# A transformer block in fp32 on one Trainium2 core: GpSimd in program order through the first attention, its factor work in pieces, and sums kept in order

## The chip, the core and the metric

The kernel runs on one core of a Trainium2 chip. A core has a matrix engine (TensorE, PE in the profile, with its weight loads as PEld), a vector engine (VectorE, DVE), an activation engine (ScalarE, ACT), a general engine (GpSimd, POOL), and a queue engine that issues the DMAs here (SyncE, SP). Each engine takes its own instructions one after the other; semaphores make one wait for another. The metric is the device time of one execution in microseconds (us). The kernel before took 2533.49 us (median of three runs, 2530.73 to 2535.2). About 0.2% of it, 5 us, is what such a measurement can tell from no change.

## The reference

The input x is 2 x 1024 x 1024 in fp32. Four parts follow one another, each on the layernorm of x and added to x:

```python
x = x + attn_a(layernorm(x))   # 32 heads of 32, causal, rotary, a prefix of 10 adapter rows
x = x + ffn(layernorm(x))      # x @ W_base.T + b, plus 8 experts of rank 16 mixed by sparsemax
x = x + attn_b(layernorm(x))   # 8 heads of 16, not causal
x = x + ffn(layernorm(x))
```

The change touches the first, whose core is

```python
q, k, v = split(einsum('btc,oc->bto', x, w_attn), 3)      # 1024 -> 3 * 1024
rotary(t) = t * cos + concat([-t[16:], t[:16]]) * sin     # q and k, per head
y = softmax(where(causal, q k^T / sqrt(32), -inf)) v
y = y + gating * softmax(q ak^T / sqrt(1024)) av          # ak, av: adapter rows through w_attn
return y @ w_proj.T
```

## The kernel before

**Stages.** `stage_a` is the first attention for both batches (about the first 1250 us). Then come its output projection, the first feed-forward part, the second attention and the last feed-forward part, one laid into the other. Only `stage_a` and the helper `Filler` are touched.

**Units and half-steps.** `attend` works off 32 units of `stage_a`: batch b (2), group g of four heads (8), half n of the 1024 queries (2). A unit needs scores twice. First `sc` = q k^T (L297), of which DVE takes the row minimum of the negated scores (L310, `nmax` and `part`), and ACT the sum of exponentials (L318); at the unit's end ACT takes a logarithm (L325) and six small DVE operations (L335 to L340, `shift`) split the shift of each row into three bf16 parts. Then, two steps later, `st` = k q^T transposed with the shift added as a bf16 matmul (L365, L367), ACT's exponential into `pt` (L478), GpSimd's causal mask on the diagonal blocks of `pt` (L374), and `y_A` += v pt (L389). `attend` runs through this in half-steps, some 290 in all, each with the `sc` of one unit and the `st` of an earlier one; both use the same two PSUM buffers in turn, so a late minimum holds up the scores behind it. The adapter scores (L708 to L726) and their small softmax are done per unit on DVE, ACT and GpSimd (`aw`, L726).

**Fill.** Between half-steps TensorE does dense work: the projections of the units to come. `Filler` holds them as generators; each `yield` says how many nanoseconds a matmul is worth (HF * COL = 870 for 128 x 512), and after each half-step `fill.run` steps the generator until `FILL_A` is paid. What is not done by the end of stage A is done behind it.

**Projections in seven products.** From group 1 on a projection of a 2 x 2 block matrix is made with seven products in place of eight (`seven`, L618), in the order 1, 6, 2, 7, 5, 4, 3, each of four matmuls (L198 or L196 in the profile, outputs `x`, `y` and `z`; `x_v`, `y_v`, `z_v` for values). Weight combinations are made by GpSimd: `factors` (s1, s2 and one in place, L608 to L610, six operations of 128 x 256) and `last_factor` (L616, two operations), which product 3 needs. Input combinations are made once for each batch: `combine` writes twelve tiles, t3 and t2 by DVE (L581, L582), t4 by GpSimd (L586), to DRAM `td`, from which a `Stream` reads them back through five buffers; `combine_first` (L600) makes another in place on GpSimd. Sums of products are taken by DVE (L636 to L654). Finished parts of q and k go to `rotate` (L770): DVE shuffle (L775), DVE times cos (L776), GpSimd times sin (L777), GpSimd add (L778), all 128 x 512.

**Order.** TensorE runs in the order in which the program is written; the others are ordered by the scheduler, where `keep_in_program_order` ties an instruction behind the one of its engine that was written before it.

Of the kernel before, what the change touches and what calls it, by code (L numbers as in the profile page):

```python
# [20 lines left out]
P = 128  # L21
# [3 lines left out]
HF = 512  # L25
# [10 lines left out]
COL = 1.7  # L36
FILL_A = 2080.0
FILL_B = 2650.0, 2200.0
# [10 lines left out]
class Filler:  # L49
# [4 lines left out]
    def __init__(self):  # L54
        self.gens = deque()
        self.done = set()
        self.debt = 0.0
        self.spent = 0.0
        self.at = {}
        self.ahead = 0  # L60

    def add(self, gen, gate=None):
        self.gens.append((gen, gate))

    def step(self, cold=True):
        while self.gens:
# [19 lines left out]
            if isinstance(r, tuple):  # L86
                self.done.add(r)
                self.at[r] = self.spent
                continue
            self.spent += r  # L90
            return r
        return None
# [44 lines left out]
def tile_model(ctx: ExitStack, tc: tile.TileContext, d, out: bass.AP):  # L137
# [379 lines left out]
    def stage_a(wk, big):  # L517
# [31 lines left out]
        def block(b, i):  # L549

            k, n = divmod(i, 10)
            return xnT[b, n - 1][:, 4 * (k - 1) : 4 * k, :]
# [21 lines left out]
        streams = {}  # L574

        def combine(b):

            for c in range(4):
                b11, b12, b21, b22 = (block(b, i)[:, c, :] for i in (11, 12, 21, 22))
                t3, t2, t4 = (big.tile([P, HF], F32, tag="tt", name=f"tn{b}_{i}_{c}") for i in (3, 2, 4))  # L580
                dve.tensor_sub(t3, b22, b12)  # L581
                dve.tensor_add(t2, t3, b11)  # L582
                sp.dma_start(td[b, 3, c], t3)
                sp.dma_start(td[b, 2, c], t2)
                for h in range(0, HF, 2 * P):
                    pool.tensor_sub(t4[:, h : h + 2 * P], t2[:, h : h + 2 * P], b21[:, h : h + 2 * P])  # L586
                sp.dma_start(td[b, 4, c], t4)

            order = []
            for g in range(NG):  # L590
                order += [2, 3, 4] if g else []
                if g > 1 or b:
                    order += [4] if g % 2 else [2, 3]
            streams[b] = Stream(b, order)

        def combine_first(b):
            for c in range(4):
                t1, b11 = block(b, 12)[:, c, :], block(b, 11)[:, c, :]
                for h in range(0, HF, 2 * P):
                    pool.tensor_sub(t1[:, h : h + 2 * P], t1[:, h : h + 2 * P], b11[:, h : h + 2 * P])  # L600

        def factors(w, tag, nm):


            s1, s2 = (wk.tile([P, 4, P], F32, tag=tag, name=f"s{i}_{nm}", bufs=2) for i in (1, 2))
            for c in range(0, 4, 2):
                cs = slice(c, c + 2)
                pool.tensor_add(s1[:, cs], w[21][:, cs], w[22][:, cs])  # L608
                pool.tensor_sub(s2[:, cs], s1[:, cs], w[11][:, cs])
                pool.tensor_sub(w[21][:, cs], w[11][:, cs], w[21][:, cs])  # L610
            return {1: w[11], 2: w[12], 3: w[12], 4: w[22], 5: s1, 6: s2, 7: w[21]}

        def last_factor(f):
            for c in range(0, 4, 2):
                cs = slice(c, c + 2)
                pool.tensor_sub(f[3][:, cs], f[3][:, cs], f[6][:, cs])  # L616

        def seven(b, nm, f, mul, shape, c, first, settled):  # L618

            stream = streams[b]
            right = {1: lambda k: block(b, 11)[:, k, :], 2: lambda k: block(b, 21)[:, k, :], 3: lambda k: block(b, 22)[:, k, :],
                     4: lambda k: stream.get(4, k), 5: lambda k: block(b, 12)[:, k, :],
                     6: lambda k: stream.get(2, k), 7: lambda k: stream.get(3, k)}

# [5 lines left out]
            yield from product(1, x, stop=False)  # L632
            act.copy(c[22], x)
            y = block_bank(shape, f"y6_{nm}", 1)
            yield from product(6, y)
            dve.tensor_add(c[12], c[22], y)  # L636
            yield from product(2, x, start=False)
            first(x)
            y = block_bank(shape, f"y7_{nm}", 1)
            yield from product(7, y)  # L640
            last_factor(f)
            dve.tensor_add(c[21], c[12], y)
            yield None
            z = block_bank(shape, f"z_{nm}")
            yield from product(5, z, stop=False)
            dve.tensor_add(c[22], c[21], z)
            settled(22)
            y = block_bank(shape, f"y4_{nm}", 1)
            yield from product(4, y)
            dve.tensor_sub(c[21], c[21], y)  # L650
            settled(21)
            yield True
            yield from product(3, z, start=False)
            dve.tensor_add(c[12], c[12], z)  # L654
            settled(12)
# [91 lines left out]
        def adapter_parts(nm, weights, n):  # L747

            ap = bank([P, n], f"ap_{nm}")
            for c in range(NC):  # L750
                i = 32 * (c % 4)
                pe.matmul(ap[i : i + 32], lhsT=adT[:, c, :], rhs=weights(c), start=(c < 4), stop=(c >= 4), skip_group_check=True)
            parts_at[nm] = wk.tile([P, n], F32, tag="qr", name=f"parts_{nm}", bufs=2)
            evac(parts_at[nm], ap)
# [15 lines left out]
        def rotate(b, g, key, n, src):  # L770
# [5 lines left out]
            dve.tensor_mul(qT, src, cos[:, cols])  # L776
            pool.tensor_mul(qr, qr, sin[:, cols])  # L777
            pool.tensor_add(qT, qT, qr)  # L778

# [480 lines left out]
    with tc.manual_schedule(engines={mybir.EngineType.PE}):  # L1260
        with tc.tile_pool(name="big", bufs=2, side="left", reuse_waits="tile") as bigp:
# [3 lines left out]
            with tc.tile_pool(name="wkA", bufs=5, side="right", reuse_waits="tile") as wk:  # L1265
                wp = stage_a(PoolOf(wk, {"pr": 6, "qk": 6, "pt": 4}), big)
            fill.drain()
# [143 lines left out]
```

## Time and profile before

| | us |
|---|---|
| three runs | 2530.73, 2533.49, 2535.2 |
| the profiled execution | 2534.4 |
| its span in the trace | 2532.7 |
| mean granted TensorE clock | 0.992 |
| stage A, 20 to 1250: TensorE busy | 1175.57 of 1230 |
| first product L777 and add L778 of q, 128 x 512 on GpSimd | 1.78 and 1.28 |
| a factor or combination, 128 x 256 on GpSimd | 0.73 to 0.89 |
| a row minimum over 512, DVE | 0.69 to 0.75 |

How to read the lines shown below. A window has its bounds, its length, then busy time and instruction count for TensorE, weight loads, DVE, ACT and GpSimd, the granted TensorE clock (1 is full speed), the DMA share and GB/s. A wait names the engine that waited, its tile and line, the engine, tile and line that it waited for, the time in all, how often, and the longest. A timeline line has its start, its duration, engine, line, operation, output <- inputs, shapes and count, and in brackets the idle time before it and what ended it.

### The profile page before, as it was taken

The page shows a single profiled execution, that of the slowest core. Times are in us where ns is not written, and L with a number is a line of the kernel's source. Part 1 is how long each engine was busy: PE and PEld are TensorE (multiplying, and loading weights), DVE is VectorE, ACT ScalarE, POOL GpSimd, SP SyncE. Part 2 cuts the span into 40 slices and gives each one's busy share as a digit, 9 for nine tenths or more (in the row PEclk, how much of TensorE's full clock was granted, in tenths as well). Part 3 has the DMA queues.
Part 4 walks back from the last instruction along what each step waited for, and adds up shares of the span by engine and source line. Part 5 has one row for each costly group of instructions (what it writes and reads, how often), then busy time and mean ns, then how long its engine had stood idle before and what let it go on. Part 6 is the DMA issues. An engine that isn't in the chain of part 4 may idle for free.

```text
span 2532.7 us, 60644 instructions
## 1 busy us (share of the span) xinstructions
PE 2448.0 (97%) x25597; PEld 1102.8 (44%) x25597; DVE 1282.1 (51%) x4036; ACT 1093.9 (43%) x2085; POOL 586.4 (23%) x840
## 2 busy tenths in 40 slices
PE   7999999999899999999999999999999999999999
PEld 4434434444354444445433445566333563333344
DVE  7665555556555555555530113357555765654243
ACT  2336656565465665556642000011354525555200
POOL 2342343333324334333200001100100101111120
PEclk9999999999999999999999999999999999999999
DMA  6532322323323333223312461121001311212121
GB/s 210 204 88 77 102 76 89 98 81 93 126 81 107 92 105 93 86 85 84 120 63 70 154 217 54 50 90 45 34 34 35 126 35 34 93 43 83 44 100 42
DMA packets 142513, 224.36 MB, mean 89 GB/s; under 512 B 12832, under 2 KB 73376, under 8 KB 142240
## 3 DMA queue, kind: packets, MB, share of 16 engines
q1 hardware_dynamic: 142240, 220.48, 27.0%
q8 instruction: 200, 3.28, 0.5%
q14 instruction: 73, 0.60, 0.1%
HBM read 168.01 MB, written 52.43 MB: 87 GB/s over the span
## 4 chain that ended last, share of the span: by engine, by line
PE 82%; DVE 6%; ACT 5%; POOL 3%; DMA 3%; issue 1%; SPq 0%; ACTq 0%; POOLq 0%; DVEq 0%
PE fo_f L196 11%; PE st L367 9%; PE fo_f L198 8%; PE sc L297 6%; PE op L196 6%; PE y_A L389 5%; PE y L198 4%; PE z L198 4%; PE op L198 3%; PE st L365 3%; PE x L198 3%; PE y_B L389 2%; PE y_v L198 2%; ACT pr_A L318 2%; PE bq L196 2%; PE z_v L198 2%
## 5 line engine op out<-in xcount | busy, mean ns | idle before, releaser
L478 ACT ACTIVATE pt<-st 128x1024 f32<-128x1024 f32 (+1 forms) x418 | 426.3, 1020 | 650.9 <-PE st L367 481.2
L318 ACT ACTIVATE pr_A<-pr_A,nmax_A 128x896 f32<-128x896 f32 (+7 forms) x512 | 390.0, 765 | 71.9 <-DVE nmax_A L310 71.5
L310 DVE CUSTOM_DVE_ANT_0 pr_A<-sc,mask 128x512 f32<-128x512 f32 (+3 forms) x512 | 250.9, 536 | 198.1 <-PE sc L297 103.4
L297 PE MATMUL sc<-kT,qT 32*128 32x512 f32 (+3 forms) x1536 | 329.4, 526 | 13.8 <-DVE nmax_A L310 8.1
L367 PE MATMUL st<-qT,kT 32*128 32x512 f32 (+3 forms) x1536 | 309.2, 489 | 0.0
L214 POOL TENSOR_TENSOR xf<-xf,b_base 128x256 f32<-128x256 f32 x128 | 89.3, 730 | 759.4 <-DVE xn_f L236 456.2
L196 PE MATMUL fo_f<-wb,xt_f 128*128 128x512 f32 x548 | 248.1, 596 | 0.4 <-ACT hwT_f L1117 0.4
L310 DVE CUSTOM_DVE_ANT_0 pr_A<-sc,mask,part_A 128x512 f32<-128x512 f32 (+1 forms) x256 | 156.1, 647 | 158.2 <-PE sc L297 100.9
L198 PE MATMUL fo_f<-wb,xt_f 128*32 128x512 f32 x1904 | 226.9, 595 | 0.1
L374 POOL TENSOR_SCALAR_AFFINE_SELECT pt<-pt 128x256 f32<-128x256 f32 x256 | 100.0, 409 | 460.3 <-ACT pt L478 460.3
L389 PE MATMUL y_A<-pt,v 128*32 128x512 f32 (+3 forms) x1536 | 166.7, 502 | 13.6 <-POOL pt L374 13.6
L318 ACT ACTIVATE pr_B<-pr_B,nmax_B 128x1024 f32<-128x1024 f32 x128 | 145.6, 1140 | 30.9 <-DVE nmax_B L310 30.8
L196 PEld LDWEIGHTS fo_f<-wb,xt_f 128*128 128x128 f32 x548 | 101.6, 193 | 111.2 <-issue 110.6
L297 PE MATMUL sc<-kq,qk 32*128 32x512 f32 x512 | 144.3, 640 | 2.7 <-DVE nmax_B L310 2.3
L367 PE MATMUL st<-rows_B,kq 32*128 32x512 f32 x512 | 144.3, 640 | 0.2 <-ACT pt L478 0.2
L196 PE MATMUL op<-wp,yt 128*128 128x512 f32 x334 | 143.9, 592 | 0.0
L228 ACT ACTIVATE lv_f<-ve_f 128x1 f32<-128x1 f32 x32 | 6.5, 203 | 315.7 <-DVE ve_f L226 315.7
L365 PE MATMUL st<-rows_A,ones 3*128 3x512 bf16 (+3 forms) x768 | 128.0, 330 | 13.5 <-DVE nmax_A L310 13.5
L367 PEld LDWEIGHTS st<-qT,kT 32*128 32x128 f32 x1536 | 133.7, 186 | 16.3 <-issue 11.3
L310 DVE CUSTOM_DVE_ANT_0 pr_B<-sc,mask,part_B 128x512 f32<-128x512 f32 x128 | 91.1, 746 | 78.8 <-PE sc L297 78.7
L297 PEld LDWEIGHTS sc<-kT,qT 32*128 32x128 f32 x1536 | 113.8, 185 | 30.9 <-DVE nmax_A L310 12.3
L365 PEld LDWEIGHTS <-ones 3*128 3x128 bf16 x768 | 36.9, 91 | 199.3 <-issue 191.9
(272 smaller groups left out, 3741.6 us busy)
## 6 DMA issues: line engine op xcount, KB each, us to landing
tt<-td SPq DMA_DIRECT2D x252, 256.0 KB, 2.8
wqk<-in_w_attnT SPq DMA_DIRECT2D x32, 512.0 KB, 5.2
xf<-x SPq DMA_DIRECT2D x32, 512.0 KB, 3.3
xa<-in_x SPq DMA_DIRECT2D x16, 512.0 KB, 6.4
wv<-in_w_attnT SPq DMA_DIRECT2D x8, 1024.0 KB, 5.4
yd<-ys SPq DMA_DIRECT2D x32, 256.0 KB, 2.5
yt<-yd SPq DMA_DIRECT2D x128, 64.0 KB, 2.0
xp<-in_x SPq DMA_DIRECT2D x32, 256.0 KB, 2.9
```

The source lines that it names most:

```text
L196: return pe.matmul(out, lhsT=lhsT, rhs=rhs, start=start, stop=stop, skip_group_check=True)
L198: pe.matmul(out[i : i + 32], lhsT=lhsT[:, i : i + 32], rhs=rhs, start=start, stop=stop, skip_group_check=True)
L214: pool.tensor_add(dst[:, i : i + 2 * P], a[:, i : i + 2 * P], b[:, i : i + 2 * P])
L228: act.activation(lv, ve, AF.Ln)
L297: yield w * COL, lambda: pe.matmul(dst[:, o : o + w], lhsT=self.qt[rows, qc : qc + P], rhs=self.kt[rows, c0 : c0 + w], start=True, stop=True)
L310: dve.tensor_tensor_reduce(pr[:, c0 : c0 + w], sc[:, i, o : o + w], m, -self.scale, BIG if c0 == 0 else self.part[:, col], ALU.add, ALU.mi ...
L318: tc.keep_in_program_order(act.activation(pr[:, :nk], pr[:, :nk], AF.Exp, bias=self.nmax[:, col], scale=-1.0, accum_out=self.sums[:, col]))
L365: yield w * COL / 4, lambda: pe.matmul(dst[:, o : o + w], lhsT=ones[three, :], rhs=self.rows[three, off : off + w], start=True, stop=False)
L367: yield w * COL, lambda: pe.matmul(dst[:, o : o + w], lhsT=self.kt[rows, kb * P : (kb + 1) * P], rhs=rhs, start=self.extra, stop=True)
L374: pool.affine_select(out=dg, in_=dg, compare_op=ALU.is_ge, fill=0.0, base=0, pattern=[[0, 2], [1, P]], channel_multiplier=-1)
L389: pe.matmul(self.y[32 * h : 32 * h + 32, off : off + w], lhsT=self.value(h, kb), rhs=pt[h // 2][:, h % 2, o : o + w], start=self.opens, st ...
L478: act.activation(pt[:, :, low_:wide_], st[:, :, low_:wide_], AF.Exp, scale=ts[0][0].scale)
```

## The change

- `Filler` gets a queue of small pieces (`chores`); after each step of dense work one of them is written out, and `flush` writes out all that are left.
- `combine`, `combine_first`, `factors` and `last_factor` put their operations into that queue. Each combined tile is made and stored as a piece of its own, and the stream is opened by the last piece. The factors come in the order s1, s1, s2, s2, and the one in place.
- In `seven` the queue is flushed before product 6 and before product 3; `last_factor` is called behind product 5, no longer behind product 7; the five sums, and DVE's t3 and t2, are kept in program order.
- `rotate` takes the two GpSimd operations in halves of 128 x 256, as four.
- `parts` gets a buffer of its own in place of one of the `qr` buffers.
- `stage_a` is built with GpSimd in program order.
- `FILL_A` goes from 2080 to 2040.

```diff
@@ -34,7 +34,7 @@
 NEG = -1e30
 BIG = 3e38
 COL = 1.7
-FILL_A = 2080.0
+FILL_A = 2040.0
 FILL_B = 2650.0, 2200.0
 SETTLE = 4500.0
 RING = 5
@@ -58,6 +58,11 @@
         self.spent = 0.0
         self.at = {}
         self.ahead = 0
+        self.chores = deque()
+
+    def flush(self):
+        while self.chores:
+            self.chores.popleft()()
 
     def add(self, gen, gate=None):
         self.gens.append((gen, gate))
@@ -88,6 +93,8 @@
                 self.at[r] = self.spent
                 continue
             self.spent += r
+            if self.chores:
+                self.chores.popleft()()
             return r
         return None
 
@@ -573,56 +580,67 @@
 
         streams = {}
 
+        def in_pieces(op):
+            def both(dst, x, y):
+                for h in range(0, HF, 2 * P):
+                    op(dst[:, h : h + 2 * P], x[:, h : h + 2 * P], y[:, h : h + 2 * P])
+            return both
+
+        def pin_sub(*a):
+            tc.keep_in_program_order(dve.tensor_sub(*a))
+
+        def pin_add(*a):
+            tc.keep_in_program_order(dve.tensor_add(*a))
+
+        def made(ts, b, i, c, op, x, y):
+            t = ts[i, c] = big.tile([P, HF], F32, tag="tt", name=f"tn{b}_{i}_{c}")
+            op(t, x, y)
+            sp.dma_start(td[b, i, c], t)
+
         def combine(b):
 
+            ts = {}
             for c in range(4):
                 b11, b12, b21, b22 = (block(b, i)[:, c, :] for i in (11, 12, 21, 22))
-                t3, t2, t4 = (big.tile([P, HF], F32, tag="tt", name=f"tn{b}_{i}_{c}") for i in (3, 2, 4))
-                dve.tensor_sub(t3, b22, b12)
-                dve.tensor_add(t2, t3, b11)
-                sp.dma_start(td[b, 3, c], t3)
-                sp.dma_start(td[b, 2, c], t2)
-                for h in range(0, HF, 2 * P):
-                    pool.tensor_sub(t4[:, h : h + 2 * P], t2[:, h : h + 2 * P], b21[:, h : h + 2 * P])
-                sp.dma_start(td[b, 4, c], t4)
+                fill.chores.append(lambda c=c, x=b22, y=b12: made(ts, b, 3, c, pin_sub, x, y))
+                fill.chores.append(lambda c=c, y=b11: made(ts, b, 2, c, pin_add, ts[3, c], y))
+                fill.chores.append(lambda c=c, y=b21: made(ts, b, 4, c, in_pieces(pool.tensor_sub), ts[2, c], y))
 
             order = []
             for g in range(NG):
                 order += [2, 3, 4] if g else []
                 if g > 1 or b:
                     order += [4] if g % 2 else [2, 3]
-            streams[b] = Stream(b, order)
+            fill.chores.append(lambda: streams.update({b: Stream(b, order)}))
 
         def combine_first(b):
             for c in range(4):
                 t1, b11 = block(b, 12)[:, c, :], block(b, 11)[:, c, :]
-                for h in range(0, HF, 2 * P):
-                    pool.tensor_sub(t1[:, h : h + 2 * P], t1[:, h : h + 2 * P], b11[:, h : h + 2 * P])
+                fill.chores.append(lambda t1=t1, b11=b11: in_pieces(pool.tensor_sub)(t1, t1, b11))
 
         def factors(w, tag, nm):
 
 
             s1, s2 = (wk.tile([P, 4, P], F32, tag=tag, name=f"s{i}_{nm}", bufs=2) for i in (1, 2))
-            for c in range(0, 4, 2):
-                cs = slice(c, c + 2)
-                pool.tensor_add(s1[:, cs], w[21][:, cs], w[22][:, cs])
-                pool.tensor_sub(s2[:, cs], s1[:, cs], w[11][:, cs])
-                pool.tensor_sub(w[21][:, cs], w[11][:, cs], w[21][:, cs])
+            for op, dst, x, y in ((pool.tensor_add, s1, w[21], w[22]), (pool.tensor_sub, s2, s1, w[11]),
+                                  (pool.tensor_sub, w[21], w[11], w[21])):
+                for c in range(0, 4, 2):
+                    cs = slice(c, c + 2)
+                    fill.chores.append(lambda op=op, dst=dst, x=x, y=y, cs=cs: op(dst[:, cs], x[:, cs], y[:, cs]))
             return {1: w[11], 2: w[12], 3: w[12], 4: w[22], 5: s1, 6: s2, 7: w[21]}
 
         def last_factor(f):
             for c in range(0, 4, 2):
                 cs = slice(c, c + 2)
-                pool.tensor_sub(f[3][:, cs], f[3][:, cs], f[6][:, cs])
+                fill.chores.append(lambda cs=cs: pool.tensor_sub(f[3][:, cs], f[3][:, cs], f[6][:, cs]))
 
         def seven(b, nm, f, mul, shape, c, first, settled):
 
 
 
-            stream = streams[b]
             right = {1: lambda k: block(b, 11)[:, k, :], 2: lambda k: block(b, 21)[:, k, :], 3: lambda k: block(b, 22)[:, k, :],
-                     4: lambda k: stream.get(4, k), 5: lambda k: block(b, 12)[:, k, :],
-                     6: lambda k: stream.get(2, k), 7: lambda k: stream.get(3, k)}
+                     4: lambda k: streams[b].get(4, k), 5: lambda k: block(b, 12)[:, k, :],
+                     6: lambda k: streams[b].get(2, k), 7: lambda k: streams[b].get(3, k)}
 
             def product(i, dst, start=True, stop=True):
                 for k in range(4):
@@ -631,27 +649,29 @@
             x = block_bank(shape, f"x_{nm}")
             yield from product(1, x, stop=False)
             act.copy(c[22], x)
+            fill.flush()
             y = block_bank(shape, f"y6_{nm}", 1)
             yield from product(6, y)
-            dve.tensor_add(c[12], c[22], y)
+            tc.keep_in_program_order(dve.tensor_add(c[12], c[22], y))
             yield from product(2, x, start=False)
             first(x)
             y = block_bank(shape, f"y7_{nm}", 1)
             yield from product(7, y)
-            last_factor(f)
-            dve.tensor_add(c[21], c[12], y)
+            tc.keep_in_program_order(dve.tensor_add(c[21], c[12], y))
             yield None
             z = block_bank(shape, f"z_{nm}")
             yield from product(5, z, stop=False)
-            dve.tensor_add(c[22], c[21], z)
+            last_factor(f)
+            tc.keep_in_program_order(dve.tensor_add(c[22], c[21], z))
             settled(22)
             y = block_bank(shape, f"y4_{nm}", 1)
             yield from product(4, y)
-            dve.tensor_sub(c[21], c[21], y)
+            tc.keep_in_program_order(dve.tensor_sub(c[21], c[21], y))
             settled(21)
             yield True
+            fill.flush()
             yield from product(3, z, start=False)
-            dve.tensor_add(c[12], c[12], z)
+            tc.keep_in_program_order(dve.tensor_add(c[12], c[12], z))
             settled(12)
             pair.rotate(1)
 
@@ -750,7 +770,7 @@
             for c in range(NC):
                 i = 32 * (c % 4)
                 pe.matmul(ap[i : i + 32], lhsT=adT[:, c, :], rhs=weights(c), start=(c < 4), stop=(c >= 4), skip_group_check=True)
-            parts_at[nm] = wk.tile([P, n], F32, tag="qr", name=f"parts_{nm}", bufs=2)
+            parts_at[nm] = wk.tile([P, n], F32, tag=f"parts{n}", name=f"parts_{nm}", bufs=1)
             evac(parts_at[nm], ap)
             return 2 * n * COL
 
@@ -774,8 +794,10 @@
             qr = wk.tile([P, HF], F32, tag="qr", name=f"{key}r{b}_{g}_{n}", bufs=2)
             dve.stream_shuffle(qr, src, [(i + HD // 2) % HD for i in range(HD)])
             dve.tensor_mul(qT, src, cos[:, cols])
-            pool.tensor_mul(qr, qr, sin[:, cols])
-            pool.tensor_add(qT, qT, qr)
+            for h in range(0, HF, 2 * P):
+                hs = slice(h, h + 2 * P)
+                pool.tensor_mul(qr[:, hs], qr[:, hs], sin[:, cols][:, hs])
+                pool.tensor_add(qT[:, hs], qT[:, hs], qr[:, hs])
 
         def begin(b, g):
 
@@ -1263,7 +1285,8 @@
             ps = psa.enter_context(tc.tile_pool(name="psA", bufs=1, space=bass.MemoryType.PSUM, reuse_waits="tile"))
             big = PoolOf(bigp, {"h16": 2, "t4k": 3, "tt": RING})
             with tc.tile_pool(name="wkA", bufs=5, side="right", reuse_waits="tile") as wk:
-                wp = stage_a(PoolOf(wk, {"pr": 6, "qk": 6, "pt": 4}), big)
+                with tc.manual_schedule(engines={mybir.EngineType.Pool}):
+                    wp = stage_a(PoolOf(wk, {"pr": 6, "qk": 6, "pt": 4}), big)
             fill.drain()
             psa.close()
             ps = ctx.enter_context(tc.tile_pool(name="ps", bufs=3, space=bass.MemoryType.PSUM, reuse_waits="tile"))
```

## The prediction

> **What bounds the kernel now.** I read the page's busy times first, then windows by stage, then TensorE's waits in stage A, then the timelines around each of them.
>
> ```profile
> PE 2448.0 (97%) x25597; PEld 1102.8 (44%) x25597; DVE 1282.1 (51%) x4036; ACT 1093.9 (43%) x2085; POOL 586.4 (23%) x840
> 20.00:1250.00 1230.00, 1175.57 (x16536) 548.89 (x16538) 698.98 (x2250) 698.05 (x1415) 429.96 (x584) 0.98 0.33 102
> 1250.00:2532.00 1282.00, 1263.27 (x9020) 546.90 (x9008) 568.16 (x1743) 390.50 (x657) 152.41 (x227) 1.00 0.21 72
> ```
>
> TensorE (first number after the length) is the bound; after 1250 us it is busy 1263.3 of 1282 at clock 1.00. Only stage A can pay: 1230 - 1175.6 = 54.4 us idle, and some time at a lower granted clock. The waits, as microseconds in all, times, longest:
>
> ```profile
> PE y_A L389 <- POOL pt L374: 13.6, 10, 2.0
> PE st L365 <- DVE nmax_A L310: 13.5, 10, 3.3
> PE sc L297 <- DVE nmax_A L310: 8.1, 8, 2.1
> PE sc L297 <- POOL qT L778: 2.1, 1, 2.1
> ```
>
> GpSimd's masks cost 13.6, the row minima 13.5 + 8.1 = 21.6. The profiled execution took 2534.4 (span 2532.7 and 1.7 around it); the median of the three runs, 2533.49, is 0.9 lower. I sum against 2534.4 and take off 0.9 at the end.
>
> **What is removed.** *Masks.* A mask stands behind other GpSimd work:
>
> ```profile
> 265.75 0.73 POOL L610 TENSOR_TENSOR wqk<-wqk 128x256 f32<-128x256 f32 x1
> 266.43 1.28 POOL L778 TENSOR_TENSOR kT<-kT,kr 128x512 f32<-128x512 f32 x1
> 267.65 0.79 POOL L374 TENSOR_SCALAR_AFFINE_SELECT pt<-pt 128x256 f32<-128x256 f32 x2
> 268.13 0.41 PE L389 MATMUL y_A<-pt,v 128*32 128x256 f32 x2 [1.39 <-POOL pt L374]
> ```
>
> In the changed program's GpSimd order the masks stand ahead of that rotary and factor work at seven of the ten places; at the others a factor had waited for its weights, which are now read later. All ten give 13.6, half of them 6.8. I take 12.0, since most waits have this one length (1.38).
>
> *Combined inputs of batch 1.* Eight DVE operations L581/L582, in one place, delay the minima: waits of 1.49 at 678.0 and 3.26 at 685.2, and the clock of 680 to 695 was 0.77, that is 0.23 x 15 = 3.4 us lost.
>
> ```profile
> 680.00:695.00 15.00, 11.74 (x80) 3.18 (x76) 6.65 (x18) 4.60 (x7) 5.82 (x8) 0.77 0.65 227
> 682.42 0.69 DVE L581 TENSOR_TENSOR tn<-xnT 128x512 f32<-128x512 f32 x1 [2.42 <-DMA td<-tn]
> 685.23 0.61 PE L365 MATMUL st<-rows_A,ones 3*128 3x512 bf16 x2 [3.26 <-DVE nmax_A L310]
> ```
>
> One operation per dense step leaves a store's 2.5 us for its buffer to come free. All: 1.49 + 3.26 + 3.4 = 8.15; at least 3. I take 8.15. The twelve stores of each batch are the same, each now issued behind its tile; the first tile is read back later, with one landing of 2.8 us as the price of no cover: I take 0, other projections lie between.
>
> *Rotary in halves.* At 619.3 and 709.5 the minima waited (2.02 + 2.15) because the small shift operations on DVE, 0.17 alone, stretched beside a rotary product; the clock of 620 to 625, 0.66, lost 0.34 x 5 = 1.7.
>
> ```profile
> 613.25 1.78 POOL L777 TENSOR_TENSOR kr<-kr,sin 128x512 f32<-128x512 f32 x1 [2.80 <-DVE m_A L335]
> 613.81 1.25 DVE L336 TENSOR_SCALAR m_A<-m_A 128x16 f32<-128x16 f32 x1
> ```
>
> Halves, four instructions at about 0.74 (rows of L609 and L616, same shape) = 2.96 for 1.78 + 1.28 = 3.06, shorten one blocking, not their sum. Bounds 0 and 5.9; I take half, 2.9. [...]
>
> *Sums in order.* Of the 21.6 us on minima, 4.75 and 4.17 are named above; 12.7 stay, of which seven waits with 8.5 follow a sum or its rotary part that DVE took ahead of the minima. With the 1.7 that 1095 to 1105 lost in clock (0.17 x 10) that is 10.2 at most, 0 at least; I take half, 5.1.
>
> Gains: 12.0 + 8.15 + 2.9 + 5.1 = 28.2, between 9.8 and 37.9.
>
> **What is added.** *The turn to batch 1.* Chores that no step has run are flushed before product 6. In the changed GpSimd order thirteen operations come between the adapter product (L726 before) of the first unit of batch 1 and the second factor of its value product 6: four of `combine_first` (0.76 each by L600) and nine factor pieces (0.73 to 0.75). That is about 9.7 us. Before, these factors ran from 616 to 645.
>
> ```profile
> 713.79 1.07 PE L198 MATMUL y_v<-s_v,tt 128*32 128x128 f32 x32
> 714.77 0.46 POOL L726 TENSOR_TENSOR aw<-ae,ad 128x160 f32<-128x160 f32 x1 [2.14 <-DVE ad L724]
> ```
>
> The factor is ready at 714.77 + 0.46 + 9.7 = 724.9, and product 6 was due at 713.8: 11.1 us idle. TensorE is in order, so every later matmul waits too; DVE, ACT and SP only catch up. For the clock: the gap of 3.26 cost 3.4. I take 11.1 + 3.4 = 14.5; 12.8 with 1.7 for the clock, 16.2 with the 5.1 that 150 to 165 lost (0.34 x 15). [...]
>
> *Product 3 of group 1.* The last factor now follows product 5, behind that product's rotary part, and the pinned sum follows a shift chain that waits for a logarithm until 144.2. Six small DVE operations until 145.55 (six of about 0.22), sum 0.69, shuffle 0.76, four GpSimd quarters 2.96, first half of the factor 0.73: 150.7.
>
> ```profile
> 145.13 3.62 PE L198 MATMUL z<-xnT,wqk 128*32 128x512 f32 x32
> 152.15 1.94 PE L297 MATMUL sc<-kT,qT 32*128 32x128 f32 x8 [2.10 <-POOL qT L778]
> ```
>
> 150.7 - 145.1 = 5.55 takes the place of the 2.10 (the clock loss of 150 to 165 stays): 3.4, between 1 and 5.
>
> *Product 3 of groups 2, 4 and 6 of batch 0.* In these the sum is pinned behind two minima of the next half-step, and two value-factor pieces stand before the last factor. Group 4: product 5 ends at 357.66 (timeline), the half-step's scores follow until 358.8, two minima until 360.3, sum 361.0, shuffle 361.75, quarters 364.7, two pieces 366.2, factor 366.9. Product 3 stood at 364.41: 2.5 late. Group 6 has the same order, 2.5. Group 2: product 5 ends at 188.5, its half-step's scores at 189.6; the same chain gives 197.7, and product 3 now comes straight after product 4, whose last piece ends near 195.9: 1.8. Sum 6.8. Of ten gaps from 1.8 to 3.3 us seven were followed by a lost 1.7 or more: 3 x 0.7 x 1.7 = 3.6. I take 10.4; bounds 0 (if the factors jump in) and 7.5 + 5.1 = 12.6. In odd groups no minimum and no piece stands ahead: in group 3 the chain of 0.69 + 0.74 + 2.96 + 0.73 = 5.1 from 278.8 fits before 285.57, with 1.6 to spare. In group 2 of batch 1 only the pieces do: 910.35 to 917.1, due 917.73.
>
> *FILL_A.* Some 290 half-steps lose 40 ns each, 11.6 us of dense work, which TensorE does after 1250 instead: 0, because it is the same work on the same engine. Thinner cover could lengthen each of some 50 waits by 0.04, 2.0 at most. The own buffer of `parts` costs nothing while it is read before the next one; without that cover one such wait, 1 us.
>
> Losses: 14.5 + 3.4 + 10.4 = 28.3, between 13.8 and 33.8 (36.8 with the last two). Sum: 2534.4 - 28.2 + 28.3 = 2534.5, less 0.9: 2533.6, say **2534**. The bounds together reach from 2533.5 - 37.9 + 13.8 = 2509 to 2533.5 - 9.8 + 36.8 = 2560.
>
> **The rivals.** *A, slower, 2542:* the minima still come late, since halves and pinned sums leave DVE the same work and the same GpSimd operations beside it; then 2.9 + 5.1 = 8.0 are not gained. For it: 2.96 against 3.06 on GpSimd. Against: the sums do stand behind the minima now. It decides once more than 5 of the 8 are missing.
>
> *B, faster, 2523:* the last factors come in time in groups 2, 4 and 6, and 10.4 are not lost. For it: group 3 has 1.6 to spare, and TensorE arrives later where it waited elsewhere. Against: the chains counted above.
>
> *C, the masks stay (the order does not do what it says), 2539:* they wait for ACT's exponentials anyway and give 6.8 instead of 12.0. Against: in the lines of 265 to 268 GpSimd was busy up to the mask.
>
> **How the numbers follow.** About 0.2% (5 us) can be told from no change here: faster is under 2528.4, slower over 2538.6. Forecast 0.36 (same 0.22, faster 0.06, slower 0.08), A 0.31 (slower 0.26, same 0.05), B 0.25 (faster), C 0.08 (slower 0.06, same 0.02). Faster 0.31, same 0.29, slower 0.40. The forecast's own range is 2528 to 2540. The wide range goes to B with another 7 of gains, 2516, and to A with 10 of the remaining bounds, 2552; what lies outside is one in five.
>
> **What would show it.** One gap of 9 to 12 us before the first value product 6 of batch 1; at most three waits of `y_A` on masks; no gap over 2 us while the combined inputs of batch 1 are made; waits of `z` on the factor (L616 before) of 5 to 6 us in group 1 and about 2 in groups 2, 4 and 6 of batch 0. I am wrong if that large gap is missing, if `z` waits in many later groups, or if the time after stage A changes by more than the 11.6 moved into it.

## The result, and the profile after

The changed kernel takes 2532.95 us (median of twelve runs, 2530.1 to 2537.43), the kernel before 2532.69 in twelve runs beside it: a ratio of 1.0002, 95% interval 0.9993 to 1.0011. Nothing moved that can be measured. Inside stage A much moved. The profiled execution of the changed kernel has a span of 2528.5 us, 4.2 less than the one shown of before, which is within the spread of single runs of either kernel.

First the busy line of the page and two windows of the changed kernel (length, then busy time and count of TensorE, weight loads, DVE, ACT, GpSimd, then clock, DMA share, GB/s):

```profile
PE 2442.0 (97%) x25477; PEld 1101.8 (44%) x25477; DVE 1273.5 (50%) x4036; ACT 1091.8 (43%) x2085; POOL 604.9 (24%) x968
20.00:1250.00 1230.00, 1173.70 (x16486) 548.85 (x16488) 693.07 (x2263) 698.90 (x1422) 448.72 (x713) 0.98 0.33 102
680.00:695.00 15.00, 15.00 (x189) 5.57 (x188) 9.48 (x32) 10.14 (x20) 7.12 (x10) 1.00 0.59 202
```

TensorE is busy 1173.7 us in stage A's window against 1175.6: about as idle as before. But 680 to 695, where the clock had been 0.77 and TensorE idle for 3.3 us, is now full at clock 1.00. GpSimd has 968 instructions in place of 840, for the halves.

Now TensorE's waits from 20 to 1250 us in the changed kernel (engine, tile, line, what it waited for, us in all, times, longest). L203 and L205 are L196 and L198 of before, L304 is L297, L317 is L310, L372 is L365, L381 is L374, L396 is L389, L629 and L635 are the factors and the last factor. (The units of stage A in fact run on until about 1390 us, beside the output projection; between 1250 and 1400 TensorE is idle for 0.3 us before and not at all after, so nothing that matters lies behind 1250.)

```profile
PE z L205 <- POOL wqk L635: 15.9, 7, 6.3
PE y_v L205 <- POOL s_v L629: 11.8, 1, 11.8
PE sc L304 <- DVE nmax_A L317: 10.2, 9, 2.3
PE st L372 <- DVE nmax_A L317: 3.3, 3, 1.8
PE sc L304 <- POOL qT L800: 1.4, 2, 0.7
PE y_A L396 <- POOL pt L381: 0.2, 1, 0.2
```

The masks (last line) went from 13.6 to 0.2, the row minima from 21.6 to 13.5. In their place stand two waits that the kernel before did not have: product 3 on the last factor, 15.9, and one value product 6 on its factor, 11.8. The single gaps of the changed kernel that make up these two, as they stand in its timeline (start, duration, instruction, in brackets the idle time before it):

```profile
145.19 5.30 PE L205 MATMUL z<-xnT,wqk 128*32 128x512 f32 x32 [6.31 <-POOL wqk L635]
197.84 1.07 PE L205 MATMUL z<-xnT,wqk 128*32 128x512 f32 x8 [2.14 <-POOL wqk L635]
360.80 1.93 PE L205 MATMUL z<-xnT,wqk 128*32 128x512 f32 x8 [3.18 <-POOL wqk L635]
519.25 1.06 PE L205 MATMUL z<-xnT,wqk 128*32 128x512 f32 x8 [3.18 <-POOL wqk L635]
```

They are groups 1, 2, 4 and 6 of batch 0, the four that the prediction named. Adding up every gap of TensorE over 0.15 us, from 20 us to the end of stage A, gives 54.2 us before and 56.0 after.

The clock has to be counted with care. One minus the clock, summed over stage A, is 18.8 us before and 23.9 after. But the clock is also low while TensorE stands idle, where it costs nothing: from 702 to 711 us of the changed kernel it is 0.50, with TensorE busy for 0.00 us. Weighted with TensorE's busy share, in steps of 1 us, the loss is 18.1 before and 16.8 after. So gaps and clock of stage A together change by 1.8 - 1.3 = 0.5 us, and the medians by 0.26. These are two single executions: their spans differ by 4.2 the other way, of which 1.6 is clock lost behind 1800 us in the one of before; the rest of the difference is not explained. The clock also differs between executions of one program: both_unpinned and best_again below are the same kernel, and their profiled executions lost 8.5 and 11.3 us in stage A by the same count.

### The profile page after: what moved, and what is told of

Same layout as the page of the kernel before. It is cut to its first block, busy times and chain, and to the rows that moved or that the text cites. A ratio compares the mean times of both kernels' runs of the same rounds, so it can differ in the third digit from the quotient of the medians.

```text
span 2528.5 us, 60549 instructions
## 1 busy us (share of the span) xinstructions
PE 2442.0 (97%) x25477; PEld 1101.8 (44%) x25477; DVE 1273.5 (50%) x4036; ACT 1091.8 (43%) x2085; POOL 604.9 (24%) x968
## 3 DMA queue, kind: packets, MB, share of 16 engines
q8 instruction: 199, 3.26, 0.5%
## 4 chain that ended last, share of the span: by engine, by line
PE 83%; DVE 6%; ACT 5%; POOL 3%; issue 2%; DMA 1%; SPq 0%; ACTq 0%; DVEq 0%; POOLq 0%
PE fo_f L203 11%; PE st L374 9%; PE fo_f L205 7%; PE sc L304 7%; PE op L203 6%; PE y_A L396 5%; PE y L205 4%; PE z L205 4%; PE op L205 3%; PE st L372 3%; PE x L205 3%; ACT pr_A L325 2%; PE y_B L396 2%; PE bq L203 2%; PE y_v L205 2%
## 5 line engine op out<-in xcount | busy, mean ns | idle before, releaser
L317 DVE CUSTOM_DVE_ANT_0 pr_A<-sc,mask 128x512 f32<-128x512 f32 (+3 forms) x512 | 251.0, 537 | 218.8 <-PE sc L304 125.8
L304 PE MATMUL sc<-kT,qT 32*128 32x512 f32 (+3 forms) x1536 | 329.2, 525 | 11.8 <-DVE nmax_A L317 10.2
L374 PE MATMUL st<-qT,kT 32*128 32x512 f32 (+3 forms) x1536 | 309.9, 490 | 0.0
L317 DVE CUSTOM_DVE_ANT_0 pr_A<-sc,mask,part_A 128x512 f32<-128x512 f32 (+1 forms) x256 | 156.5, 648 | 192.3 <-PE sc L304 132.2
L203 PE MATMUL fo_f<-wb,xt_f 128*128 128x512 f32 x558 | 251.3, 593 | 0.4 <-ACT hwT_f L1139 0.4
L205 PE MATMUL fo_f<-wb,xt_f 128*32 128x512 f32 x1864 | 221.9, 595 | 0.0
L381 POOL TENSOR_SCALAR_AFFINE_SELECT pt<-pt 128x256 f32<-128x256 f32 x256 | 99.7, 408 | 483.3 <-ACT pt L485 483.3
L396 PE MATMUL y_A<-pt,v 128*32 128x512 f32 (+3 forms) x1536 | 160.3, 500 | 0.2 <-POOL pt L381 0.2
L203 PEld LDWEIGHTS fo_f<-wb,xt_f 128*128 128x128 f32 x558 | 102.9, 192 | 112.8 <-issue 112.2
L304 PE MATMUL sc<-kq,qk 32*128 32x512 f32 x512 | 144.3, 640 | 3.2 <-DVE nmax_B L317 2.8
L203 PE MATMUL op<-wp,yt 128*128 128x512 f32 x338 | 145.7, 592 | 0.0
L374 PE MATMUL st<-rows_B,kq 32*128 32x512 f32 x512 | 144.3, 640 | 0.0
L374 PEld LDWEIGHTS st<-qT,kT 32*128 32x128 f32 x1536 | 134.0, 186 | 16.6 <-issue 11.6
L372 PE MATMUL st<-rows_A,ones 3*128 3x512 bf16 (+3 forms) x768 | 128.2, 330 | 3.3 <-DVE nmax_A L317 3.3
L317 DVE CUSTOM_DVE_ANT_0 pr_B<-sc,mask,part_B 128x512 f32<-128x512 f32 x128 | 91.2, 747 | 79.7 <-PE sc L304 79.7
L304 PEld LDWEIGHTS sc<-kT,qT 32*128 32x128 f32 x1536 | 113.4, 184 | 28.7 <-DVE nmax_A L317 13.3
L372 PEld LDWEIGHTS <-ones 3*128 3x128 bf16 x768 | 36.4, 91 | 190.9 <-issue 183.5
```

The source lines that it names most:

```text
L203: return pe.matmul(out, lhsT=lhsT, rhs=rhs, start=start, stop=stop, skip_group_check=True)
L205: pe.matmul(out[i : i + 32], lhsT=lhsT[:, i : i + 32], rhs=rhs, start=start, stop=stop, skip_group_check=True)
L304: yield w * COL, lambda: pe.matmul(dst[:, o : o + w], lhsT=self.qt[rows, qc : qc + P], rhs=self.kt[rows, c0 : c0 + w], start=True, stop=True)
L317: dve.tensor_tensor_reduce(pr[:, c0 : c0 + w], sc[:, i, o : o + w], m, -self.scale, BIG if c0 == 0 else self.part[:, col], ALU.add, ALU.mi ...
L372: yield w * COL / 4, lambda: pe.matmul(dst[:, o : o + w], lhsT=ones[three, :], rhs=self.rows[three, off : off + w], start=True, stop=False)
L374: yield w * COL, lambda: pe.matmul(dst[:, o : o + w], lhsT=self.kt[rows, kb * P : (kb + 1) * P], rhs=rhs, start=self.extra, stop=True)
```

## The experiments

Twelve runs of ten kernels, each timed in several rounds beside the kernel before: best_again is both_unpinned once more, whole_rotary_again is best_whole_rotary. The ratios are to the kernel before, with 95% intervals.

| kernel | median us | ratio |
|---|---|---|
| turn_early | 2520.80 | 0.9954 (0.9940 to 0.9969) |
| last_early | 2513.05 | 0.9923 (0.9909 to 0.9938) |
| both_early | 2503.76 | 0.9885 (0.9871 to 0.9900) |
| both_unpinned | 2497.57 | 0.9854 (0.9838 to 0.9871) |
| after_unpinned | 2510.93 | 0.9915 (0.9895 to 0.9935) |
| best_whole_rotary | 2499.97 | 0.9872 (0.9848 to 0.9897) |
| best_combine_at_once | 2500.77 | 0.9871 (0.9855 to 0.9886) |
| best_gpsimd_scheduled | 2518.57 | 0.9931 (0.9906 to 0.9955) |
| best_again | 2498.93 | 0.9862 (0.9847 to 0.9878) |
| turn_early_unpinned | 2500.54 | 0.9875 (0.9862 to 0.9888) |
| whole_rotary_again | 2497.97 | 0.9864 (0.9847 to 0.9881) |
| fill_2080 | 2492.51 | 0.9837 (0.9824 to 0.9851) |

### The turn to batch 1: turn_early

```diff
@@ project_first
             for n in range(2):
+                if b and n == 0:
+                    yield from begin(1, 1)
+                    yield from begin_values(1, 0)
...
@@ project
-            if ng and nb < B:
+            if ng and nb < B and (nb, ng) != (1, 1):
...
@@ values
-            if (b, g) == (1, 0):
-                yield from begin_values(b, g)
```

> The changed kernel with one edit: the factors of group 1 and of the first value block of batch 1 are queued at the first step of batch 1's first projection, before its products, and no longer behind it. In the trace of the changed kernel TensorE waited 11.8 us before the first value product 6 of batch 1 (start 711.3), and the clock of 700 to 715 was 0.66, 0.50 and 0.50, which is 6.7 us lost. Theory (this stall is a loss of its own, which cancels the gains): both go, 2532.95 - 18.5 = 2514.5, between 2512 and 2519. Rival (the stall gave ACT and DVE time to catch up and hid waits that now come back, as the 2.15 us at 709 of the kernel before with its clock): at most two thirds are gained, 2521 or more. Second rival (the order of GpSimd leaves the factors late all the same): no change, 2530 or more.

It measured 2520.8, 12.1 us less than the changed kernel: next to the bound of the rival, and short of the theory's 18.5. By the time alone the rival would stand; the trace decides against it. The gap of 11.8 is gone, between 619 and 769 us no wait of TensorE over 0.3 us has come back, and the sum of gaps falls from 56.0 to 45.7. So the stall was a loss of its own. What was wrong is the clock in the expectation. This is GpSimd in the changed kernel during the gap, and then two windows of that trace:

```profile
701.91 0.47 POOL L746 TENSOR_TENSOR aw<-ae,ad 128x160 f32<-128x160 f32 x1
702.33 2.78 POOL L586 TENSOR_TENSOR xnT<-xnT,xnT 128x256 f32<-128x256 f32 x4
705.05 1.42 POOL L629 TENSOR_TENSOR s<-wqk 128x256 f32<-128x256 f32 x2
706.41 1.42 POOL L629 TENSOR_TENSOR s<-s,wqk 128x256 f32<-128x256 f32 x2
707.77 1.43 POOL L629 TENSOR_TENSOR wqk<-wqk 128x256 f32<-128x256 f32 x2
709.13 1.43 POOL L629 TENSOR_TENSOR s_v<-wv 128x256 f32<-128x256 f32 x2
710.49 1.44 POOL L629 TENSOR_TENSOR s_v<-s_v,wv 128x256 f32<-128x256 f32 x2
```

```profile
699.00:712.00 13.00, 1.19 (x36) 0.87 (x28) 0.92 (x3) 0.95 (x4) 13.00 (x22) 0.60 0.01 2
711.00:715.00 4.00, 3.71 (x46) 2.44 (x48) 0.00 (x0) 0.00 (x0) 2.30 (x4) 0.50 0.14 38
```

GpSimd does not pause once: it is busy 13.0 of 13 us, with the queue of pieces flushed behind the adapter product, in the order counted before. TensorE is busy 1.19 of those 13 us, so nearly all of the half rate there is free. Only from 711.3 to 715 does it cost: 0.5 x 3.7 = 1.9 us, in place of the 6.7 of the expectation. 56.0 - 45.7 + 1.9 = 12.2, against 12.1 measured; of the stall's 11.8, 1.5 stand again as small gaps far from the turn, most of it a wait of 1.16 near 103 us that also differs between the two executions of both_unpinned's kernel.

### The place of the last factor: last_early, both_early

```diff
             yield from product(7, y)
+            last_factor(f)
...
             yield from product(5, z, stop=False)
-            last_factor(f)
```

> The changed kernel with one edit: the last factor's two pieces are queued behind product 7 again, as before the change, instead of behind product 5. The changed kernel's trace shows 6.31, 2.14, 3.18 and 3.18 us of waits of product 3 on the last factor (groups 1, 2, 4 and 6 of batch 0), and about 1.1 in three later ones; the clock lost around 140-155, 360-370 and 520 is 3.4 + 3.4 + 1.7 = 8.5. Theory: the 15.9 us and most of the clock go, but the wait for the rotary part of q in group 1 (2.1 us before the change, with 5.1 of clock) returns: 2532.95 - 15.9 - 8.5 + 7.2 = 2516, between 2511 and 2522. Rival (the sums pinned behind the minima are what is late, and the waits only move from the factor to the rotary parts or to the scores): half or less, 2525 or more.

2513.05: 19.9 us less than the changed kernel, as the theory said (2511 to 2522). In its trace no wait of `z` on L635 is left, and the rotary wait of group 1 is back as two, 1.39 and 1.44:

```profile
PE y_v L205 <- POOL s_v L629: 11.8, 1, 11.8
PE sc L304 <- DVE nmax_A L317: 9.4, 9, 2.2
PE sc L304 <- POOL qT L800: 4.2, 4, 1.4
```

> Both edits in one kernel. Theory (the two losses lie in different places and add up): the gains of the two single edits add, about 2532.95 - 18.5 - 17 = 2497.5, between 2492 and 2505; faster than both kernels by 1.1 to 1.6%. Rival (waits that take the place of the removed ones): less than three quarters of the sum of the two single gains.

2503.76, 29.2 us less than the changed kernel, where the two single gains make 12.1 + 19.9 = 32.0: nine tenths of it. The losses lie in different places, and both kernels are beaten, though the time stands inside the expected 2492 to 2505 only at its upper end.

### The order of the sums: both_unpinned, after_unpinned, turn_early_unpinned

```diff
-            tc.keep_in_program_order(dve.tensor_add(c[22], c[21], z))
+            dve.tensor_add(c[22], c[21], z)
```

and so for the other four sums.

> As both_early, but the five sums of each projection are not kept in program order. The prediction gave the order of the sums a gain of 5.1 us (0 to 10.2). Theory: 5 us slower than both_early, with the waits of the scores on row minima back near the 12.7 us that the kernel before had outside the turn to batch 1. Rival A of the prediction (the minima come late anyway): within 2 us of both_early. Third reading (pinning makes sums and rotary parts late): faster than both_early by 2 us or more.

2497.57 against 2503.76: the third reading, faster by 6.2 us, and no execution of either reaches into the other's range. Pinning (keeping a sum in program order, here also called tying it) costs time. Where it is supposed to help, it gains a microsecond at most. The waits on minima in the changed kernel are 10.2 + 3.3 = 13.5, shown above; in the changed kernel without pins (after_unpinned) they are:

```profile
PE sc L304 <- DVE nmax_A L317: 8.1, 7, 2.3
PE z L205 <- POOL wqk L635: 4.9, 5, 3.0
PE st L372 <- DVE nmax_A L317: 4.9, 6, 1.8
```

8.1 + 4.9 = 13.0, or 14.2 with two waits of 0.59 on the half-way minimum `part_A`, which only the kernel without pins has; and product 3 waits 4.9 instead of 15.9.

> The changed kernel itself, with the five sums not kept in program order (GpSimd's order stays the same, instruction by instruction). The prediction took 5.1 us of gain from the pins and charged the pinned sums with the late last factors (3.4 in group 1 and 10.4 in groups 2, 4 and 6). Theory, from both_unpinned against both_early (6.2 us faster): without the pins the sums run earlier, so most of the 14.8 us of waits of product 3 in those four groups go, and the time is 2533 - 14.8 + 2.1 - 3 of clock, about 2517, between 2512 and 2525. Rival (the place of the last factor behind the rotary part is what makes it late, not the pins): 2527 or more.

2510.93, 22.0 us less than the changed kernel with one edit that takes nothing but five ties away: more than the theory gave. In its profiled execution the gaps fall from 56.0 to 45.6, and the clock lost while TensorE is busy from 16.8 to 6.9, where the theory had 3. The changed kernel shows at group 4 how the ties work. First the end of product 5 on TensorE, then DVE (start, duration, instruction):

```profile
348.80 1.90 PE L205 MATMUL z<-xnT,s 128*32 128x512 f32 x16
351.81 0.75 DVE L317 CUSTOM_DVE_ANT_0 pr_A<-sc,mask,part_A 128x512 f32<-128x512 f32 x1 [2.13 <-PE sc L304]
352.48 0.74 DVE L317 CUSTOM_DVE_ANT_0 pr_A<-sc,mask,part_A 128x512 f32<-128x512 f32 x1
353.15 0.68 DVE L665 TENSOR_TENSOR qT<-qT,z 128x512 f32<-128x512 f32 x1
353.88 0.72 DVE L795 STREAM_SHUFFLE qr<-qT 128x512 f32<-128x512 f32 x1
```

and GpSimd from there:

```profile
354.68 1.25 POOL L799 TENSOR_TENSOR qr<-qr,sin 128x256 f32<-128x256 f32 x1 [11.24 <-DVE qr L795]
356.01 0.74 POOL L800 TENSOR_TENSOR qT<-qT,qr 128x256 f32<-128x256 f32 x1
356.70 0.74 POOL L799 TENSOR_TENSOR qr<-qr,sin 128x256 f32<-128x256 f32 x1
357.52 0.73 POOL L800 TENSOR_TENSOR qT<-qT,qr 128x256 f32<-128x256 f32 x1
358.21 1.41 POOL L629 TENSOR_TENSOR wv<-wv 128x256 f32<-128x256 f32 x2
359.57 1.86 POOL L635 TENSOR_TENSOR wqk<-wqk,s 128x256 f32<-128x256 f32 x2
```

Product 5 ends at 350.70. Its sum (L665) runs 2.4 us later, behind two minima whose scores were not there yet: DVE was idle until 351.81. GpSimd has been idle for 11.24 us, and could have made the last factor at once: its factor s2 had been made before product 6, and product 2, the last reader of the tile it changes, was long over. In program order it is held behind the rotary part of that sum. So a tie on one engine becomes a wait on a second that has nothing to do, and then on TensorE (360.80, 3.18 us). Most of the 11.24 comes from the place of the last factor, behind product 5, and 2.4 from the tie. Without ties (after_unpinned) the rotary part of the same sum follows the end of product 5, at 343.93, by 1.62 us in place of 3.98, and product 3 of group 4 does not wait:

```profile
342.03 1.90 PE L205 MATMUL z<-xnT,s 128*32 128x512 f32 x16
345.55 1.24 POOL L799 TENSOR_TENSOR qr<-qr,sin 128x256 f32<-128x256 f32 x1 [8.85 <-DVE qr L795]
```

> both_unpinned with the last factor behind product 5, where the change put it. Theory (the place of the last factor alone is nearly free once the sums are not pinned: after_unpinned keeps 4.9 us of waits on it of 15.9): 3 to 6 us slower than best_again. Rival (it is the place that matters and after_unpinned only hid it behind the 11.8 us stall): 10 us slower or more.

0.9875 against 0.9862 of best_again on the same chip, 3 us (1.6 by the medians), with intervals that overlap: at the small end of the theory, and not told from nothing; the rival's 10 us are excluded. Either edit, no pins or an earlier last factor, takes most of the same loss away. Their gains do not add (19.9 and 22.0 alone, 35.4 for all three edits).

### The parts that were to gain

All three start from both_unpinned.

```diff
@@ best_whole_rotary
-            for h in range(0, HF, 2 * P):
-                hs = slice(h, h + 2 * P)
-                pool.tensor_mul(qr[:, hs], qr[:, hs], sin[:, cols][:, hs])
-                pool.tensor_add(qT[:, hs], qT[:, hs], qr[:, hs])
+            pool.tensor_mul(qr, qr, sin[:, cols])
+            pool.tensor_add(qT, qT, qr)
@@ best_combine_at_once
                     combine(b)
+                    if b:
+                        fill.flush()
@@ best_gpsimd_scheduled
-                with tc.manual_schedule(engines={mybir.EngineType.Pool}):
+                if True:
                     wp = stage_a(PoolOf(wk, {"pr": 6, "qk": 6, "pt": 4}), big)
```

> As both_unpinned (2497.57, ratio to before 0.9854), but the two GpSimd operations of the rotary part are 128 x 512 again, two in place of four. The prediction gave the halves 2.9 us (0 to 5.9). Theory: slower than both_unpinned by 2 to 6 us, ratio 0.9862 to 0.9878, with longer waits of the scores on row minima near 600 and 710 us. Rival A (the same sum of GpSimd time beside DVE, so the same waits): ratio within 0.0008 of 0.9854.

> best_whole_rotary again, whose interval could not tell a loss from none. In the trace of both_unpinned the six small DVE operations near 594 took 0.66 to 0.79 each beside halves, where two took 1.25 and 1.12 beside whole operations, and the wait at 599 is 2.31 (2.02 before the change). Rival A (the same sum): within 2 us of best_again. Theory of the prediction: 2 to 6 us slower; the wait at 96 us, 3.99 there against 2.50, would be where.

The first could not tell (0.9872, 0.9848 to 0.9897). The second, beside best_again, gave 0.9864 against 0.9862: no difference, though intervals of this width do not exclude the 2.9 us either. The gaps are the closer measure: in the two executions with whole operations they add up to 30.8 and 30.6 us, in the two with halves to 29.9 and 30.6. The wait near 95 to 99 us is indeed longer with whole operations (3.99 and 3.11 against 2.50 and 2.06), but most of that is lost again at other places. So the halves gain at most about 1 us. The reason is in the small shift operations. Of the six, four run beside the rotary products; here they are in whole_rotary_again with the wait behind them, and then, after the same sum, in best_again with halves:

```profile
596.55 1.29 DVE L344 CAST shift<-m_A 128x16 bf16<-128x16 f32 x1
597.88 1.28 DVE L345 TENSOR_TENSOR m_A<-m_A,shift 128x16 f32<-128x16 f32 x1
599.19 0.34 DVE L346 CAST shift<-m_A 128x16 bf16<-128x16 f32 x1
599.57 0.23 DVE L347 TENSOR_TENSOR shift<-m_A,shift 128x16 bf16<-128x16 f32 x1
601.19 0.58 PE L304 MATMUL sc<-kT,qT 32*128 32x128 f32 x2 [2.49 <-DVE nmax_A L317]
```

```profile
598.25 0.74 DVE L344 CAST shift<-m_A 128x16 bf16<-128x16 f32 x1
599.02 0.76 DVE L345 TENSOR_TENSOR m_A<-m_A,shift 128x16 f32<-128x16 f32 x1
599.82 0.66 DVE L346 CAST shift<-m_A 128x16 bf16<-128x16 f32 x1
600.51 0.79 DVE L347 TENSOR_TENSOR shift<-m_A,shift 128x16 bf16<-128x16 f32 x1
602.69 0.38 PE L304 MATMUL sc<-kT,qT 32*128 32x128 f32 x2 [2.29 <-DVE nmax_A L317]
```

Beside two whole operations two of them take 1.29 and 1.28 us, beside four halves all four take 0.66 to 0.79, one for each half that GpSimd begins: 3.14 in sum against 2.95, and the wait behind them 2.49 against 2.29. In both_unpinned, the same kernel as best_again, the four take 0.74, 0.77, 0.66 and 0.79 and end at 595.28, 596.08, 596.77 and 597.60 us; GpSimd's four halves take 1.24, 0.74, 0.73 and 0.72 and end at 595.22, 596.03, 596.72 and 597.52. So each ends 0.05 to 0.08 us behind a half. At 138 us of the changed kernel, where GpSimd is idle, the same four take 0.18 to 0.23. What these lines show is that this chain of dependent small operations loses one such time at every link.

> As both_unpinned, but the twelve combined tiles of batch 1 are all queued and written out in one place, as the kernel before had them. The prediction gave the pieces 8.15 us (3 to 8.15): two waits on row minima of 1.5 and 3.3 us, and 3.4 us of clock. Theory: 4.8 to 8.2 us slower than both_unpinned, ratio 0.9873 to 0.9886, and the waits back in this stage. Rival (the order of GpSimd and not the pieces took these waits away): ratio within 0.0008 of 0.9854.

0.9871 against 0.9854, 4 us, just under the theory, and outside the 2 us of the rival; the two intervals overlap, and against best_again (0.9862), the same kernel once more, it is only 2. The time alone does not decide. The trace does: between 655 and 667 us the waits are back, smaller, where both executions of both_unpinned's kernel have none from 640 to 690:

```profile
PE st L372 <- DVE nmax_A L317: 3.2, 2, 1.7
```

3.2 us in place of 4.75, and the clock there stayed at 1.

> As both_unpinned, but stage A is built without GpSimd in program order, so that the scheduler places its instructions. The prediction gave that order 12.0 us (6.8 to 13.6) for the ten waits of y_A on masks. Theory: the masks wait again, 12 us slower than both_unpinned, ratio 0.990. Rival (the pieces and the places where they are written, not the order, keep the masks clear): ratio within 0.002 of 0.9854.

0.9931 against 0.9854. The four times of this kernel lie between 2508 and 2519, so the size of the loss is rough: 10 to 21 us. The mean granted clock was 0.998 in the shortest and 0.993 to 0.994 in the three others, and 0.4 to 0.5% of 2506 us, 10 to 13 us, covers the 10 to 11 between them. The profiled execution, the shortest, with a span of 2506.3, shows the masks:

```profile
PE y_A L396 <- POOL pt L381: 13.8, 8, 1.9
```

as in the kernel before, 13.6. It is the program order of GpSimd that keeps them clear.

### The share of dense work: fill_2080

```diff
-FILL_A = 2040.0
+FILL_A = 2080.0
```

> both_unpinned again, on the chip of the next three, with more rounds: a ratio to the kernel before near 0.9854.

> best_again with FILL_A at 2080. The prediction: the same work at another place, 0, and 0 to 2 us of difference in the waits. Theory: within 2 us of best_again. Rival (more cover per half-step lets minima and factors come in time, or crowds DVE): 3 us or more to either side.

best_again: 0.9862, as before. fill_2080: 2492.51, ratio 0.9837, 6.4 us less than best_again by the medians. Its times lie between 2488.51 and 2493.48, those of best_again between 2491.89 and 2499.64; the two intervals of the ratio overlap at their ends. The sums of gaps are the same (30.0 and 30.6 us). The clock lost while TensorE is busy is 7.9 us against 11.3 in the two profiled executions, 3.4 us. Over all their executions the mean granted clock was 0.996 to 0.998 against 0.994 to 0.997, so most of the difference goes with the clock. Whether the share of fill brought that about, or chance, as between the two executions of both_unpinned's kernel, is not shown. This is the fastest kernel of the study, 1.6% below both.

## Why the prediction was right

The forecast was no change at 2534; it measured 2532.95. The sum held, and most of its terms; two were wrong. The chances leaned another way than the sum: slower had 0.40, no change 0.29.

*Right in place and nearly in size.* Masks: 12.0 taken, 13.4 by the trace. The turn to batch 1: a gap of 11.1 was worked out, it is 11.81, by the operations that were counted. Product 3 of group 1: 5.55 worked out, 6.31 measured. Groups 2, 4 and 6: 1.8, 2.5 and 2.5 worked out, 2.14, 3.18 and 3.18 measured. The chains were right; what they missed is that GpSimd's operations stretched beside DVE's product with cos (1.25 above for the first rotary quarter, beside the product at 354.64, where 0.74 was put in, and 1.86 for the two pieces of the last factor, beside the product at 359.27, where two of 0.73 make 1.46).

*Right in place, wrong in size.* The clock behind the turn: 3.4 taken, 1.9 in the trace. The combined inputs: 8.15 taken. The 4.75 of gaps and the low clock of 680 to 695 are gone, but undone alone they cost 2 to 4 us, near the lower bound of 3. Whether the clock falls behind such a gap is not fixed: in the kernel before it fell behind seven of the ten gaps of 1.78 to 3.26 us, and behind the gap of 2.66 near 47 us, where 3.0 us were lost, it stayed at 1.00 in the changed kernel.

*Wrong: the halves.* 2.9 taken, at most about 1 by the gaps. The step "shorten one blocking, not their sum" was right (3.14 us whole against 2.95 in halves above), and half of 5.9 should not have been taken on top of it. Of the two waits named there, that at 619 is still 2.02. The one at 709 lay behind the new stall, and did not return when the stall was taken away, with halves or with whole operations; why was not tried.

*Wrong: the sums in order.* 5.1 of gain taken, measured a microsecond at most on the minima (13.5 with ties, 13.0 to 14.2 without). The prediction did charge the ties, together with the new place of the last factor, with late last factors, 3.4 + 10.4 = 13.8, a balance of 8.7 lost; taking the ties alone away gives 22.0, and the new place alone 19.9.

*Why the sum still held.* The two terms that failed are 8.0 of gain, of which 2 came at most: rival A's mechanism, and it took place. Rival A's time did not, as other terms gave it back: 1.4 at the masks, the 2.15 at 709, 1.6 in the first unit (1.93 and 2.98 before, 2.26 and 1.04 now), and the clock. Against these stand 2.5 us of longer gaps at the four product 3, 0.7 at the turn, 1.1 at three later product 3, and a new wait of 1.83 of the adapter product at 159. Split up, the terms had gaps 1.7 shorter and clock 1.9 longer; the traces have gaps 1.8 longer and clock 1.3 shorter. So the balance came out by some 3 us of clock, as much as differs between two executions of one program (8.5 and 11.3 above): that the total met the forecast to 1 us is luck. That gains and losses of some 25 us each would cancel is not: the large ones stand in the traces where the prediction put them. Rival B fell with the waits of groups 2, 4 and 6, rival C with the masks' 0.2. FILL_A was taken as 0 with 2 at most; on the kernel without ties the medians differ by 6, with intervals that touch and most of it clock.

## What to carry to other kernels

An order that is fixed on one engine passes every delay of its first instruction to all that stands behind, also to work whose inputs are ready (in group 4 a sum that ran 2.4 us late held back a last factor that could have been made, and TensorE waited 3.18): before tying an instruction, look what is queued behind it on the engines that wait for it. Work that is due early belongs ahead of work that can be late; a queue that is flushed when its content is needed hides this until the flush, here until a stall of 11.8 us. When a change brings nothing, list its waits one by one: here three edits of a few lines, found that way, turned no change into 1.4 to 1.5%.

## What had not been expected of the hardware

The granted clock also fell while TensorE was idle, and this part was free: in the gap before 711.3 us it stood at 0.50 for some 9 us, and the loss behind the gap of 11.8 was 1.9 us, about as much as the 1.7 behind a gap of 2.26 (96 us) and less than the 3.1 behind one of 3.18 (361 us). A sum of one minus the clock over time counted 23.9 us where 16.8 were lost.

Splitting two GpSimd operations into halves hardly freed DVE's chain of four small operations beside them: 1.29, 1.28, 0.34 and 0.23 us, 3.14 in sum (whole_rotary_again), became 0.74, 0.76, 0.66 and 0.79, 2.95 (best_again).
